# Half 0 of a mixing step computed by blocks of 16 rows instead of units of 8, with whole PSUM banks

## The chip, the core and the metric

The kernel runs on one core of one Trainium2 chip. The metric is the time of one execution on the device in microseconds (us); the figure for a version is the median of its runs. The core has five engines that run side by side, each with its own instruction stream: TensorE (PE, matrix products into PSUM), VectorE (DVE), ScalarE (ACT), GpSimd (POOL) and SyncE (SP, which here only issues DMA transfers). An engine waits for another by a semaphore.

## The reference

The function takes an image `x` of 256 rows x 256 columns x 128 channels and runs two layers on it, each as `x + layer(groupnorm(x))`. Layer 0 is gated attention along each row. Layer 1 treats the 256 rows of the first axis as 256 *tokens*, each an image of 256 x 128 pixels, and does this, cut to what matters here:

```python
tok_n = instance_norm(tokens)
k, q  = fno_layer(tok_n, ...), fno_layer(tok_n, ...)   # low resolution
v     = fno_layer(tok_n, ...)                          # full resolution
probs = softmax(q k^T)                                 # 8 heads, 256 x 256 each
attn  = probs v                                        # tokens mixed, every pixel
attn  = fno_layer(attn, p_wr, p_wi, p_bias, p_sw, p_sb)
attn  = instance_norm(attn + tokens)
...                                                    # two more FNO layers on groups of 4 tokens
```

An `fno_layer` is a 1 x 1 skip product plus a product in a few low Fourier modes, turned back into an image. The kernel has folded the attention heads, the value and output skips and the residual into one 256 x 256 matrix over the tokens (`mpT`), and all that passes through modes into a small set of modes (`Gd0`, in DRAM). What the stage of the change computes is therefore

    y = rwb * (mpT . x1 + inverse transform of the modes Gd0)

for all 256 tokens and all 32768 pixels, and, for each token, the statistics (mean and variance) of y, which the next normalisation needs. `x1` is the output of layer 0, `rwb` a row of 128 factors over the image column.

## The kernel before

Layer 0 takes about the first 1650 us of the execution and isn't touched. Layer 1 works on two halves of 128 tokens, half 0 and half 1, with one token per partition. After the attention matrix is made, `y_blocks(0, ...)` computes y of half 0 and leaves it in SBUF (`blocks`, 16 blocks of 2048 pixels a token; `hb[b]` is block b). Then the first spectral stage of half 0 (`first_modes`) runs interleaved with `y_blocks(1, ...)`, which computes y of half 1 and stores it to DRAM (`yd`). The later stages follow.

All of this is in a `manual_schedule`: on each engine the instructions stand in the order in which the Python code issues them, SP's DMAs among them. Nothing is reordered by a scheduler. Tiles come from pools; a tile with `bufs=3` has three buffers that are used in turn, and an instruction that takes a buffer over waits until the last reader of its former content is done.

A *unit* u of `y_blocks` is 8 rows of the 256 x 128 image (1024 pixels); a block is two units. For each unit:

- `load(u + 2)` issues on SP the DMAs of unit u + 2: x1 of both token halves, `xt`, 2 x 512 KB, three buffers (`load_x1`, L1017), and for an even unit the modes of its block, `gs`, 4 x 64 KB, three buffers (`load_modes`, L1248).
- Four PSUM tiles `yps_..._j` are taken from a pool of 8 banks of 512 columns (pool `psy`). Each uses the first 256 columns of its bank. Tile j holds the rows n with n mod 4 = j (`by_turn`).
- Mixing matmuls (L1351): for each j and each token half sc one product of `mpT` (128 x 128) with 256 pixels of `xt`. They use the whole 128 x 128 array. In the profile each appears as two instructions, so a unit has 16.
- `image` (L1219): for each of the unit's two rows per tile, and each j, the inverse transform along one row, of 32 modes into 128 columns. These matmuls use a row tile of 32 of the array; the four j use four different tiles. Again 16 instructions a unit in the profile.
- DVE multiplies each of the four tiles by `rwb` into `blocks` (L1361, 128 x 256 each) and takes the statistics of the unit's 1024 pixels in two `bn_stats` (L1363, 512 each).

When all 32 units are done, the pool `psy` is closed, and its banks pass to the pool `pz`, from which `y_blocks(1, br, ...)` and `first_modes` take theirs (four banks each). The first DVE instruction of `first_modes` is the aggregate of the statistics (`bn_aggr`, L1451). The image matmuls of later stages come from the same function `image`, there with four rows at a time, as do `first_images` (tiles `ups`) and `output` (tiles `h2ps`).

## Time and profile before

| | |
|---|---|
| median of 3 runs | 2884.54 us (2880.02 to 2887.79) |
| profiled execution | 2878.79 us, of it the span of the profile 2877.0 us |
| mean granted TensorE clock | 0.957 |
| busy in the span: PE, DVE, POOL, ACT | 92%, 70%, 58%, 52% |
| half 0 of y, first matmul to first matmul of half 1 | 1892.67 to 2032.05 us |

The span runs from the first to the last instruction of the profiled execution. All times inside it are counted from its start. The page divides it into 40 slices of 72 us and gives for each the busy share of an engine in tenths (9 is 90% or more); the stage of the change lies in slices 27 to 29:

```profile
PE   7799999999999999999999989999889988799655
DVE  7788888888888888888888854756645555365445
ACT  0477777777777777777777622200004611365132
POOL 0399999999999999999999900200114733111211
PEclk9999999999999999999999999999999999799865
DMA  9422222222222222222222101188879984798599
```

`DMA` is the mean busy share of the 16 DMA engines. The matmuls are pipelined, and their ends are modelled, so what tells the pace of PE is when one group starts after another, not the busy time of one. In lines of the costs and the timeline, "x16" is the number of instructions, and the time in brackets is how long the engine stood idle before the first of them, with what ended it.

### The profile page before, as it was taken

What the parts mean: (1) busy time and instruction counts of PE and PEld (TensorE: products, weight loads), DVE (VectorE), ACT (ScalarE), POOL (GpSimd) and SP (SyncE); (2) the same over time, 40 slices, a digit from 0 to 9 for tenths busy, and PEclk for the clock granted to TensorE, in tenths of its full rate; (3) what the DMA queues carried; (4) which work ended last, traced back from release to release, by engine and by line L of the source; (5) the groups of instructions that cost most, each with busy time, mean ns of one, the idle gap of its engine ahead of it and who ended that gap; (6) DMA issues with size and microseconds to landing.
All of it is one profiled execution on the core that took longest, in us unless ns stands there. A gap on an engine that the chain in (4) does not pass through costs nothing. (4 is left out here: it accounts for less than half of the span.)

```text
span 2877.0 us, 71481 instructions
## 1 busy us (share of the span) xinstructions
PE 2643.1 (92%) x29116; PEld 1935.1 (67%) x29116; DVE 2004.2 (70%) x3264; ACT 1488.4 (52%) x2847; POOL 1679.6 (58%) x1308
## 2 busy tenths in 40 slices
PE   7799999999999999999999989999889988799655
PEld 6677777777777777777777656778665555455533
DVE  7788888888888888888888854756645555365445
ACT  0477777777777777777777622200004611365132
POOL 0399999999999999999999900200114733111211
PEclk9999999999999999999999999999999999799865
DMA  9422222222222222222222101188879984798599
GB/s 369 166 67 67 67 67 67 67 67 67 68 67 67 67 67 67 67 67 67 67 67 67 47 22 54 34 276 274 281 243 312 311 304 134 253 363 306 187 360 339
DMA packets 246705, 430.12 MB, mean 149 GB/s; under 512 B 26278, under 2 KB 174201, under 8 KB 239976
## 3 DMA queue, kind: packets, MB, share of 16 engines
q1 hardware_dynamic: 206568, 335.34, 35.4%
q0 software_dynamic: 22912, 81.80, 7.4%
q10 hardware_dynamic: 16896, 8.39, 1.0%
q8 instruction: 231, 3.78, 0.6%
q14 instruction: 98, 0.80, 0.1%
HBM read 290.17 MB, written 135.27 MB: 148 GB/s over the span
## 5 line engine op out<-in xcount | busy, mean ns | idle before, releaser
L332 POOL TENSOR_TENSOR e<-e,b1T 128x1024 f32<-128x1024 f32 x256 | 606.1, 2367 | 164.6 <-PE u L381 90.3
L336 POOL TENSOR_TENSOR es<-e 128x512 f32<-128x512 f32 x512 | 639.6, 1270 | 20.1
L314 ACT ACTIVATE sc<-sc,b2T 128x512 f32<-128x512 f32 x512 | 339.0, 662 | 364.6 <-PE sc L305 356.2
L356 DVE RECIPROCAL av<-av 128x256 f32<-128x256 f32 x256 | 452.3, 1767 | 27.2 <-DVE og L355 1.4
L314 ACT ACTIVATE e<-sc,b2T 128x512 f32<-128x512 f32 x512 | 348.6, 681 | 0.0
L327 DVE TENSOR_TENSOR e<-sc,b1T 128x1024 f32<-128x1024 f32 x256 | 311.0, 1215 | 0.0
L305 PE MATMUL sc<-qkT 32*128 32x256 f32 x4096 | 293.4, 400 | 1.3 <-DVE e L327 1.3
L344 PE MATMUL av<-e,v 128*32 128x256 f32 x4096 | 274.7, 385 | 0.5 <-POOL e L332 0.5
L305 PEld LDWEIGHTS sc<-qkT 32*128 32x128 f32 x4096 | 185.1, 184 | 112.2 <-issue 97.7
L1351 PE MATMUL yps<-xt,mpT 128*128 128x256 f32 x1024 | 241.8, 389 | 19.4 <-DVE yt L1361 9.7
L355 DVE SCALAR_TENSOR_TENSOR og<-gate,av 128x256 f32<-128x256 f32 x256 | 107.7, 421 | 190.6 <-PE av L349 190.6
L1351 PEld LDWEIGHTS yps<-xt,mpT 128*128 128x128 f32 x1024 | 191.9, 192 | 56.7 <-DVE yt L1361 13.0
L1365 POOL DMA_DIRECT2D yd<-yt x32 | 17.7, 555 | 340.8 <-DVE yt L1361 340.8
L360 POOL TENSOR_TENSOR x<-xt,bo 128x256 f32<-128x256 f32 x256 | 187.7, 734 | 0.0
L279 PE MATMUL qk<-xnT,wT_wq 128*128 128x256 f32 x512 | 179.5, 432 | 1.7 <-ACT xnT L271 1.7
L285 PEld LDWEIGHTS gv<-wT_wv,kvT 128*128 128x128 f32 x1024 | 155.0, 192 | 13.3
L349 PE MATMUL av<-es,ones 128*32 128x256 f32 x2048 | 157.5, 379 | 2.5 <-POOL es L336 2.5
L366 PE MATMUL wo<-wT_wo,og 128*128 128x128 f32 x1024 | 156.8, 276 | 2.7 <-DVE og L357 2.7
L344 PEld LDWEIGHTS av<-e,v 128*32 128x32 f32 x4096 | 107.0, 109 | 76.1 <-POOL e L332 1.0
L381 PE MATMUL u<-adft,x 128*128 128x129 f32 x1024 | 156.4, 275 | 0.0
L285 PE MATMUL gv<-wT_wv,kvT 128*128 128x128 f32 x1024 | 156.0, 275 | 0.0
L1718 ACT ACTIVATE blocks<-h2ps,col 128x512 f32<-128x512 f32 x128 | 89.0, 779 | 129.4 <-PE h2ps L1219 129.4
(546 smaller groups left out, 5282.8 us busy)
## 6 DMA issues: line engine op xcount, KB each, us to landing
xt<-x1d SPq DMA_DIRECT2D x128, 512.0 KB, 5.9
xb<-in_x_dram SPq DMA_DIRECT2D x32, 1024.0 KB, 7.8
xt<-in_x_dram SPq DMA_DIRECT2D x128, 256.0 KB, 2.7
kt<-in_L_conv_kv_x_dram SPq DMA_DIRECT2D x128, 256.0 KB
x1d<-x SPq DMA_DIRECT2D x256, 128.0 KB, 2.3
y<-yd SPq DMA_DIRECT2D x62, 512.0 KB, 8.9
gs<-Gd SPq DMA_DIRECT2D x384, 64.0 KB, 5.1
yd<-yt POOLq DMA_DIRECT2D x32, 512.0 KB, 6.3
```

Source lines behind the costliest of these rows:

```text
L279: nc.tensor.matmul(ps[:, 0:256], wT["wq"], xnT, start=True, stop=True)
L285: nc.tensor.matmul(ps[:, 256 + c * P : 256 + (c + 1) * P], kvT[:, c * P : (c + 1) * P], wT["wv"], start=True, stop=True,)
L305: nc.tensor.matmul(sc[h // 2][:, h % 2, c * 256 : (c + 1) * 256], qkT[p, 256 + c * P : 256 + (c + 1) * P], qkT[p, 0:256], start=True, stop ...
L314: nc.scalar.activation(r["e"][1][:, :, c, :] if hp else z, z, AF.Exp, bias=b2T[:, c, s : s + 1])
L327: nc.vector.tensor_tensor(r["e"][0].rearrange("p h c q -> p (h c q)"), r.pop("sc").rearrange("p h x -> p (h x)"), b1T[:, 0:2].rearrange("p ...
L332: nc.gpsimd.tensor_tensor(e1, e1, b1T[:, 2:4].rearrange("p h c q -> p (h c q)"), ALU.mult)
L336: nc.gpsimd.tensor_tensor(r["es"][hp], e[:, :, 0, :], e[:, :, 1, :], ALU.add)
L344: nc.tensor.matmul(ps[hd, 0:256], r["v"][:, c, hd], r["e"][h // 2][:, h % 2, c, :], start=(c == 0), stop=(c == 1),)
L349: nc.tensor.matmul(ps[32 * h : 32 * h + 32, 256:512], self.ones, r["es"][h // 2][:, h % 2, :], start=True, stop=True,)
L356: nc.vector.reciprocal(rd, rd)
L360: nc.gpsimd.tensor_tensor(r["x1"], r["x"], bc(self.bo, 1, 2), ALU.add)
L1351: nc.tensor.matmul(rows_of(ps[j]), mpT[:, sc, tt], by_turn(xt[:, sc])[:, j], start=(sc == 0), stop=False,)
```

## The change

`y_blocks(0, ...)` is replaced by a function of its own for half 0, which works by blocks of 16 rows:

- A block takes four PSUM tiles of 512 columns, whole banks. The mixing matmuls of its first unit write columns 0 to 255 of each, those of its second unit columns 256 to 511. Only the very first product into a bank has the start flag.
- `image` then runs once a block over all four rows of each tile.
- DVE multiplies four tiles of 128 x 512 a block and takes the four `bn_stats` after them. The number of products falls from 128 to 64; the number of `bn_stats` stays 64.
- The modes of block b + 1 are requested at the start of block b, ahead of the x loads of units 2b + 2 and 2b + 3. Before, they were requested behind the x load of the first of these. The number and the size of the DMAs are the same.
- There are as many matmuls as before, on the same operands. Half 1 still uses `y_blocks`.

```diff
+        def y_half_0(psum):
+
+            tt = slice(0, P)
+            gss = {}
+
+            def modes(b):
+                gss[b] = xp.tile([P, 4, P], FP, tag="gs", name=f"gs_0_{b}", bufs=3)
+                load_modes(gss[b], Gd0, b, tt)
+
+            modes(0)
+            for b in range(16):
+                if b < 15:
+                    modes(b + 1)
+                for u in (2 * b + 2, 2 * b + 3):
+                    if u < 32 and (0, u) not in xts:
+                        xts[0, u] = load_x1(0, u)
+                gs = gss.pop(b)
+                ps = [psum.tile(f"yps_0_{b}_{j}") for j in range(4)]
+                for s in range(2):
+                    xt = xts.pop((0, 2 * b + s))
+                    for j in range(4):
+                        for sc in range(2):
+                            nc.tensor.matmul(
+                                rows_of(ps[j])[:, 2 * s : 2 * s + 2], mpT[:, sc, tt], by_turn(xt[:, sc])[:, j],
+                                start=(s == 0 and sc == 0), stop=False,
+                            )
+                image(ps, gs, bsy)
+                for j in range(4):
+                    nc.vector.tensor_tensor(by_turn(hb[b])[:, j], rows_of(ps[j]), bc(rwb, 1, 4), ALU.mult)
+                for g in range(4):
+                    nc.vector.bn_stats(ystat[:, 0, 4 * b + g, :], hb[b][:, g * 512 : (g + 1) * 512])
+
@@
             with tc.tile_pool(name="psy", bufs=8, space=PSUM) as psy:
-                run(y_blocks(0, Banks(psy, "y"), 0, 32))
+                y_half_0(Banks(psy, "y"))
```

In the changed file the lines of half 0 are L1390 (mixing matmuls), L1396 (the product on DVE) and L1398 (the statistics), and all lines below the new function stand 32 further down.

## The prediction

> **What bounds the kernel now.** One core, so the page and its 40 slices come first, to find where the change lies. Then the waits and the costs by line of that stretch, then the timeline of two of its units, then the timeline of its end, and last the transfers.

> The changed code runs from 1892.67 us (the first L1351 matmul) to 2032.05 us (the first matmul of half 1). In the busy times by stretch this stage reads:

> ```profile
> 1892.67:2030.55 137.88, 137.88 (x1024) 111.77 (x1024) 84.25 (x188) 0.00 (x0) 0.00 (x0) 1.00 0.87 278
> ```

> The columns are length, then busy us for each engine, the granted clock, the DMA share. PE is busy in all of the 137.88 us at full clock. DVE works 84 of them, ACT and POOL nothing. So PE sets the pace here, with DMA (87%) next. The waits of the same stretch say the same:

> ```profile
> DVE blocks L1361 <- PE yps L1219: 52.6, 32, 4.1
> PEld yps L1219 <- issue: 10.6, 32, 0.3
> PEld yps L1351 <- DVE blocks L1361: 1.7, 1, 1.7
> PE yps L1351 <- DVE blocks L1361: 1.5, 1, 1.5
> ```

> DVE waits for PE in each of the 32 units. PE waits for DVE once, at the end, and never for a transfer. The second line is the one to remember: at the start of each unit's image matmuls the weight load stands still for 0.33 us, 32 times. The timeline shows one unit:

> ```profile
> 1927.10 3.72 PE L1351 MATMUL yps<-xt,mpT 128*128 128x256 f32 x16
> ...
> 1930.75 0.54 PEld L1219 LDWEIGHTS yps<-bsy,gs 32*128 32x128 f32 x16 [0.33 <-issue]
> 1930.76 0.73 PE L1219 MATMUL yps<-bsy,gs 32*128 32x128 f32 x16
> 1930.86 5.11 SPq L1017 DMA_DIRECT2D xt<-x1d  x4
> 1931.41 3.32 PEld L1351 LDWEIGHTS yps<-xt,mpT 128*128 128x128 f32 x16
> 1931.41 3.72 PE L1351 MATMUL yps<-xt,mpT 128*128 128x256 f32 x16
> ```

> A unit takes 4.31 us: mixing matmuls (L1351) from 1927.10, image (L1219) from 1930.76, the next unit's mixing from 1931.41. So the mixing phase is 3.66 us and the image phase 0.65 (the trace counts each matmul of the source twice, hence 16). Each x load is issued 0.10 us after the mixing matmuls of the unit that held its buffer end.

> [...] The mixing matmuls use the whole array (128*128), the image ones four row tiles (32*128), so each unit switches twice. [...] The trace has 416 (L1361) and 687 (L1192, 128x512 from PSUM), and these are used. [...]

> **The change, part by part.**

> *Fewer mode switches (gain).* A block of two units now runs 32 mixing instructions, then 32 image ones: one pair of switches where there were two. What a pair costs follows from two undisturbed rows. Just ahead of the stage, L1187 runs the same 128*128 128x256 matmuls without a switch, and its DVE consumer starts each 8 of them:

> ```profile
> 1887.52 0.69 DVE L1192 TENSOR_TENSOR Fy<-Z,fyps 128x512 f32<-128x512 f32 x1 [1.04 <-PE fyps L1187]
> 1889.25 0.69 DVE L1192 TENSOR_TENSOR Fy<-Z,fyps 128x512 f32<-128x512 f32 x1 [1.04 <-PE fyps L1187]
> ```

> 1.73 us for 8 is 0.216 each. Sixteen would take 3.45, the unit takes 3.66: 0.21 us go to the two ends. For the image side, first_images runs it with four rows:

> ```profile
> 2214.08 1.17 PE L1219 MATMUL ups<-k_bsyn,gs 32*128 32x128 f32 x32
> 2215.18 1.96 PE L1572 MATMUL htps<-ident,blocks 128*128 128x128 f32 x16
> ```

> 1.10 us from its start to the next whole-array matmul, against 2 x 0.65 = 1.30: 0.20 less. After the change a block should take 2 x 3.66 - 0.21 + 1.10 = 8.21 us in place of 8.62: 0.41 us saved, times 16 blocks = 6.6 us. Bounds: if long runs don't keep the 0.216 spacing, only the image side stays, 16 x 0.20 = 3.2; if the 0.33 us idle of the weight load and 0.17 at the way back all go, 8.0. I take 6.6, for both rows are the same shapes.

> *Whole banks (DVE).* Per block 4 products of 128x512 replace 8 of 128x256. Four of 416 ns run in 1.42 us, so each starts 0.33 after the last, 0.08 less than its duration. Four of 687 should take 3 x 0.60 + 0.69 = 2.5 us, and the four statistics 2 x 1.29 = 2.58 as before: 5.1 against 5.42 us in a block of 8.21. PE hides it: 8 banks hold two blocks, so a block's banks have a whole block's 8.2 us to come free. Gain and cost nothing, except at the end.

> *The end of the stage (cost).* There nothing covers DVE:

> ```profile
> 2030.57 1.42 DVE L1361 TENSOR_TENSOR blocks<-yps,rwb 128x256 f32<-128x256 f32 x4 [1.57 <-PE yps L1219]
> ...
> 2032.05 3.72 PE L1351 MATMUL yps<-xt,mpT 128*128 128x256 f32 x16 [1.49 <-DVE blocks L1361]
> 2033.35 1.89 DVE L1451 BATCH_NORM_AGGREGATE col<-ystat 128x2 f32<-128x384 f32 x1
> ```

> The pool of half 1 takes over the banks of psy, and its first matmul starts 0.06 us after the last of the four products, not after the first: it waits for all. With 2.5 us in place of 1.42 the wait grows by 1.1. Behind the products stand four statistics instead of two (+1.29), then the aggregate (1.89): it ends 4.5 us after PE's restart, where half 1's first products, at 2036.44 us in the same timeline, could start at 4.39. About 0.1 us passes on to PE, which reuses those banks. Together -1.2. Bounds: 0, if banks are handed on one by one, to 2.4, if PE felt the statistics as well.

> *Loads.* SP issues the same DMAs in a new order: modes of block b+1, then x of units 2b+2 and 2b+3; before, the modes stood behind the even x load. The modes now wait behind the odd load of the block before, issued when a unit's mixing ends; their four issues (1.85 us) fit into the 3.45 until the next x buffer is freed, and they are asked for more than 15 us before use. So they delay no x load. But the time from freed buffer to use changes: before, each x load had two units and an image, 9.3 us. Now an even unit has 1.10 + 8.21 = 9.3, an odd one 3.45 + 1.10 + 3.55 = 8.1. Does a load take that long?

> ```profile
> 1926.55:1927.41 0.86, 0.86 (x17) 0.73 (x18) 0.22 (x1) 0.00 (x0) 0.00 (x0) 1.00 0.05 19
> ...
> 1934.29:1935.15 0.86, 0.86 (x8) 0.48 (x7) 0.00 (x0) 0.00 (x0) 0.00 (x0) 1.00 0.79 324
> 1935.15:1936.01 0.86, 0.86 (x17) 0.74 (x18) 0.20 (x1) 0.00 (x0) 0.00 (x0) 1.00 0.11 43
> ```

> Each of these stretches ends in its DMA share and GB/s. At both ends of 8.6 us the DMA engines are nearly idle (0.05, 0.11), just before an even load starts moving, so all issued earlier has landed, the odd load of 1930.86 within 4.4 us. Both leads suffice. Per block they work 0.87 x 8.62 = 7.5 us, and 8.21 is still more.

> *Sum.* 6.6 - 1.2 = 5.4 us. The profiled execution took 2878.8 us (span 2877.0 and 1.8 around it) and would take 2873.4. The median of three is 2884.5, 5.7 above it within a spread of 7.8, so the median after should be 2879.1.

> **The rivals.**

> *The gain is lost further on (0.13): 2884.5.* For it: the DMA share is 0.93 from 2190 to 2305 us and 0.99 from 2480 to 2630, so work that starts earlier could meet a resource that doesn't. Against: those transfers are issued into buffers that PE's progress frees, none starts before this stage, so they move with it.

> *More than forecast (0.10): 2875.* The switch saves the upper bound 8.0 and the end costs nothing, and a little more comes from transfers that interleave better later. For it only that the bounds allow it.

> *Slower: x arrives late (0.09): 2895.* From block 1 on, each odd unit waits for its x because the lead is 8.1 in place of 9.3 us. "No wait before" alone would allow a landing of up to 9.3. At 9.2 each of 15 blocks stalls 1.1 us: 16 us lost, less the 5.4. It decides from a stall of 0.36 us a block. The idle slices speak against it: landing would have to double because the modes now follow the odd load.

> **How the numbers follow.** The forecast has 0.68, with an own range of 2876 to 2884 (3.2 - 2.4 to 8.0 - 0). The range must also hold the spread of such medians and the first two rivals: 2871 to 2888 leaves out the slow case and some tail. A measurement of this kernel tells 0.3%, 8.7 us, from no change, so the forecast itself lies within "same". Faster by more: the second rival and 0.08 of the forecast's upper end, 0.18. Slower by more: the third rival and 0.01, 0.10. Same: 0.72.

> **What would show it.** Right: block period 8.2 us; the 0.33 us idle of the weight load 16 times in half 0, not 32; L1396 at about 687 ns x64; PE's wait for DVE at the end 2.6 us; the stage 131 us and half 1 starting near 2026.3. Wrong: PE waiting on a DMA of xt in odd units, a mixing phase above 7.2 us, or the stages after half 0 longer by as much as this one is shorter.

## The result, and the profile after

The changed kernel takes 2878.12 us (median of 22 runs, 2871.28 to 2885.2); the kernel before took 2882.3 us over as many runs. The ratio is 0.9985 with a 95% interval of 0.9978 to 0.9992: 4.3 us less, somewhere between 2.3 and 6.3.

The profiled execution of the changed kernel took 2885.2 us (span 2883.4), more than the one of before, although the median is lower. Single spans differ by more than the change is worth. So stages are compared here, each counted from its own start. Half 0 begins at 1895.43 us in the new trace. Its busy times, with the columns as in the prediction (length; busy us of PE, PEld, DVE, ACT, POOL with counts; granted clock; DMA share; GB/s):

```profile
1895.43:2026.70 131.27, 131.27 (x1024) 111.65 (x1024) 74.71 (x122) 0.00 (x0) 0.00 (x0) 1.00 0.91 291
```

131.3 us where there were 137.9, and PE is still busy in all of them. The timeline of one block (start, busy us, engine, line, operation, operands, count) shows why:

```profile
1928.23 7.17 PE L1390 MATMUL yps<-xt,mpT 128*128 128x256 f32 x32
1928.32 2.48 DVE L1396 TENSOR_TENSOR blocks<-yps,rwb 128x512 f32<-128x512 f32 x4 [3.22 <-PE yps L1219]
1930.83 2.47 DVE L1398 BATCH_NORM_STATS2 ystat<-blocks 128x6 f32<-128x512 f32 x4
...
1935.33 1.17 PE L1219 MATMUL yps<-bsy,gs 32*128 32x128 f32 x32
...
1936.44 7.17 PE L1390 MATMUL yps<-xt,mpT 128*128 128x256 f32 x32
```

From 1928.23 to 1936.44 is 8.21 us for a block; the mixing phase lasts 7.10 us, the image phase 1.11. DVE is done with a block 5.1 us after its image and then waits 3.2 us for the next. The waits of the stage (us in total, times, longest):

```profile
DVE blocks L1396 <- PE yps L1219: 56.2, 16, 8.0
PEld yps L1219 <- issue: 6.0, 18, 0.3
...
PEld yps L1351 <- DVE blocks L1396: 2.7, 1, 2.7
PE yps L1351 <- DVE blocks L1396: 2.6, 1, 2.6
```

The weight load's idleness of 0.33 us is there 16 times for half 0 (the other two belong to half 1), and PE waits for no transfer. The wait at the end has grown from 1.5 to 2.6 us, as forecast. What follows it was not forecast:

```profile
2026.81 2.48 DVE L1396 TENSOR_TENSOR blocks<-yps,rwb 128x512 f32<-128x512 f32 x4 [3.22 <-PE yps L1219]
2029.32 2.47 DVE L1398 BATCH_NORM_STATS2 ystat<-blocks 128x6 f32<-128x512 f32 x4
...
2029.35 5.41 PE L1351 MATMUL yps<-xt,mpT 128*128 128x256 f32 x16 [2.56 <-DVE blocks L1396]
2031.83 1.89 DVE L1483 BATCH_NORM_AGGREGATE col<-ystat 128x2 f32<-128x384 f32 x1
...
2034.68 0.73 PE L1219 MATMUL yps<-bsy,gs 32*128 32x128 f32 x16
```

The first unit of half 1 needs 5.33 us from its first matmul to its image (2029.35 to 2034.68). Before, it needed 3.65. No idleness stands inside it. The busy times by stretch tell what happened:

```profile
2028.00:2029.35 1.35, 0.01 (x1) 0.01 (x1) 1.32 (x4) 0.00 (x0) 0.00 (x0) 1.00 1.02 410
2029.35:2030.50 1.15, 1.15 (x3) 0.97 (x4) 1.15 (x2) 0.00 (x0) 0.00 (x0) 0.59 1.04 347
2030.50:2031.50 1.00, 1.00 (x4) 0.73 (x4) 1.00 (x3) 0.00 (x0) 0.00 (x0) 0.50 0.76 120
2031.50:2032.50 1.00, 1.00 (x4) 0.82 (x3) 0.96 (x2) 0.00 (x0) 0.00 (x0) 0.50 0.10 29
2032.50:2033.50 1.00, 1.00 (x5) 0.84 (x4) 1.00 (x1) 0.00 (x0) 0.00 (x0) 0.77 0.08 21
```

The granted clock (third number from the end) is 1.00 during the pause, falls to 0.50 at 2029.55 us, 0.2 us after PE starts again, and comes back 3.41 us later, at 2032.96. In that time the mixing instructions start 0.43 us apart (2029.77, 2030.19, 2030.62), twice the 0.22 us of full clock. PE's own speed, not a wait, costs the 1.68 us. The busy share of PE shows nothing of it: PE is busy throughout. After the end of half 0, then, two costs stand against the gain: the longer wait, and the half clock behind it.

### The profile page after: what moved, and what is told of

It is laid out like the page before. It is cut to its first block, busy times and chain, and to the rows that moved or that the text cites. A ratio compares the mean times of both kernels' runs of the same rounds, so it can differ in the third digit from the quotient of the medians.

```text
span 2883.4 us, 71403 instructions
## 1 busy us (share of the span) xinstructions
PE 2647.9 (92%) x29116; PEld 1943.0 (67%) x29116; DVE 1999.8 (69%) x3200; ACT 1487.9 (52%) x2847; POOL 1682.3 (58%) x1308
## 5 line engine op out<-in xcount | busy, mean ns | idle before, releaser
L291 DVE COPY v<-gv 128x256 f32<-128x256 f32 x256 | 108.6, 424 | 68.8 <-PE gv L289 68.8
L289 PE MATMUL gv<-xnT,wT_wg 128*128 128x256 f32 x512 | 153.4, 381 | 0.0
```

## The experiments

All times of this table are counted from the first mixing matmul of half 0. "Unit 0, length" is the time from the first matmul of half 1 to the image of that unit; "clock" is the mean granted clock over this time (over the first 4 us of it, it is 0.57 in the changed kernel, and this is the figure in the expectations below). Units 1 and 2 are the next two of half 1; "spectral" is the first `rhops` matmul of `first_modes`, which needs the aggregate of the statistics; "ups" is the first image matmul of `first_images` (tiles `ups`). The ratio is to the kernel before, run on the same chip.

| version | half 1 starts | unit 0, length | clock | unit 1 starts | unit 2 starts | spectral | ups | ratio [95%] |
|---|---|---|---|---|---|---|---|---|
| before | 139.38 | 3.65 | 1.00 | 144.25 | 150.06 | 159.63 | 298.63 | |
| changed | 133.92 | 5.33 | 0.68 | 140.48 | 146.29 | 155.86 | 299.47 | 0.9985 [0.9978, 0.9992] |
| e1_image_by_unit | 140.43 | 3.65 | 1.00 | 145.31 | 151.12 | 160.69 | 299.25 | 1.0003 [0.9992, 1.0015] |
| e2_modes_behind | 133.91 | 5.34 | 0.68 | 140.47 | 146.29 | 155.86 | 294.08 | 0.9984 [0.9974, 0.9995] |
| e8_pe_kept_busy | 133.96 | 3.62 | 1.00 | 138.81 | 144.62 | 154.20 | 292.43 | 0.9982 [0.9973, 0.9990] |
| e4_last_by_unit | 133.25 | 3.65 | 1.00 | 138.13 | 143.94 | 153.51 | 291.90 | 0.9973 [0.9960, 0.9986] |
| e6_no_seam | 131.29 | 3.65 | 1.00 | 136.74 | 141.62 | 157.01 | 294.21 | 0.9970 [0.9958, 0.9982] |
| e9_last_by_unit_no_seam | 131.70 | 3.65 | 1.00 | 136.78 | 142.59 | 152.18 | 290.71 | 0.9966 [0.9954, 0.9979] |

The theory at the start: the switches between the two tile shapes (128\*128 and 32\*128) carry the whole gain, and the end of the stage gives part of it back, by the wait and by the clock. The rivals: the gain comes from elsewhere (whole banks on DVE, the order of the DMAs), or the slow unit is slow for another reason than PE's pause.

**Is it the switches?** e1_image_by_unit keeps the change but runs the image of each unit behind that unit's mixing.

```diff
                 for s in range(2):
                     ...
+                    for k in (2 * s, 2 * s + 1):
+                        for j in range(4):
+                            q = slice(32 * j, 32 * j + 32)
+                            nc.tensor.matmul(
+                                ps[j][:, k * W : (k + 1) * W], gs[q, k, :], bsy[q, :], start=False, stop=(k == 3)
+                            )
-                image(ps, gs, bsy)
```

> The changed kernel, with the image matmuls of each unit set back behind that unit's mixing matmuls; whole banks, four 128x512 products a block and the modes one block ahead stay. Theory (the gain is the switch of the array's tiling mode, once a block in place of twice): a block takes 8.6 us again, half 0 some 138 us up to the wait at its end, the weight load idles 0.33 us 32 times in half 0, and PE still waits 2.6 us at the end; the time is 1 us above the kernel before, ratio 1.000 to 1.001. Rival (the gain is the whole banks or the earlier modes): a block stays at 8.2 us, ratio 0.9985.

The ratio is 1.0003 [0.9992, 1.0015]: all the gain is gone. Its timeline:

```profile
2025.84 3.72 PE L1390 MATMUL yps<-xt,mpT 128*128 128x256 f32 x16
...
2029.49 0.73 PE L1397 MATMUL yps<-bsy,gs 32*128 32x128 f32 x16
...
2030.15 3.72 PE L1390 MATMUL yps<-xt,mpT 128*128 128x256 f32 x16
...
2033.80 0.73 PE L1397 MATMUL yps<-bsy,gs 32*128 32x128 f32 x16
...
2037.08 3.72 PE L1351 MATMUL yps<-xt,mpT 128*128 128x256 f32 x16 [2.56 <-DVE blocks L1401]
...
2040.73 0.73 PE L1219 MATMUL yps<-bsy,gs 32*128 32x128 f32 x16
```

4.31 us a unit again, 8.62 a block, and the weight load's 0.33 us 32 times again:

```profile
PEld yps L1397 <- issue: 10.6, 32, 0.3
```

So the switches are the gain, and the whole banks by themselves cost the 1.05 us by which half 1 starts later than before (140.43 against 139.38). One thing did not fit: PE pauses for the same 2.56 us here, yet unit 0 takes 3.65 us at full clock. The last section returns to it.

**Are the earlier modes worth anything?** e2_modes_behind puts them back behind the even x load.

```diff
-                if b < 15:
-                    modes(b + 1)
                 for u in (2 * b + 2, 2 * b + 3):
                     if u < 32 and (0, u) not in xts:
                         xts[0, u] = load_x1(0, u)
+                    if u % 2 == 0 and b < 15:
+                        modes(b + 1)
```

> The changed kernel with the modes of the next block requested behind the even x load, as the kernel before had it; all else as changed. Theory (the order of the loads is worth nothing, both leads suffice): a block takes 8.21 us, half 0 lasts 134 us from its first matmul to the first of half 1, no PE wait for a transfer in half 0; ratio to before 0.998 to 0.999 like the changed kernel. Rival (the earlier modes give part of the gain): PE waits for gs in half 0 and the stage is over 135 us.

```profile
1927.62 7.17 PE L1390 MATMUL yps<-xt,mpT 128*128 128x256 f32 x32
...
1935.83 7.17 PE L1390 MATMUL yps<-xt,mpT 128*128 128x256 f32 x32
```

8.21 us a block, half 1 at 133.91 instead of 133.92, ratio 0.9984: the order of the loads is worth nothing. The half clock is there again (5.34 us).

**Is the slow unit slow because PE paused?** e8_pe_kept_busy fills the pause with five products (ten instructions) into a PSUM bank of their own, whose result nobody reads.

```diff
+            warm = psum.tile("warm")
+            for k in range(5):
+                nc.tensor.matmul(warm[:, 0:256], ident, mpT[:, k % 2, :], start=True, stop=True)
```

> The changed kernel with five matmuls of 128x256 more (ten instructions, some 2.2 us) into a free bank behind the last image matmuls of half 0; their result isn't used. Theory (PE's clock halves because PE idles 2.56 us there): the granted clock stays at 1.0 over the end of the stage and the first unit of half 1 takes 3.65 us from its first matmul to its image in place of 5.33; the start of half 1 moves by at most 0.2 us. Rival (that unit is slow for its x, its modes or by chance): it takes 5.3 us as in the changed kernel. Total: 1.7 us less than the changed kernel, or the same.

```profile
2027.66 2.43 PE L1401 MATMUL warm<-mpT,ident 128*128 128x256 f32 x10
...
2030.33 3.69 PE L1351 MATMUL yps<-xt,mpT 128*128 128x256 f32 x16 [0.25 <-PE warm L1401]
...
2033.95 0.73 PE L1219 MATMUL yps<-bsy,gs 32*128 32x128 f32 x16
```

```profile
2030.33:2033.95 3.62, 3.62 (x16) 2.93 (x16) 3.58 (x5) 0.00 (x0) 0.00 (x0) 1.00 0.76 196
```

Half 1 starts at the same place (133.96), for DVE frees the banks no sooner, but the clock stays at 1.00 and unit 0 takes 3.62 us. DVE works beside it as before (3.58 of 3.62 us). So neither DVE nor the transfers slow the unit; the clock does. That the filling is what kept the clock at 1.00, this run alone doesn't show: the pause, left empty, might have been harmless here, as it was in e1 (see the last section). Unit 1 starts 1.67 us earlier than in the changed kernel. The ratio, 0.9982, can't be told from 0.9985: 1.7 us is 0.06%, less than either interval is wide. What is shown, is shown by the profile.

**Is the end worth repairing?** e4_last_by_unit keeps blocks 0 to 14 and does block 15 in two units, with 256-column products and two `bn_stats` each, so that DVE has only 1.42 us of products behind the last image.

```diff
-            for b in range(16):
+            for b in range(15):
...
+            for s in range(2):
+                xt = xts.pop((0, 30 + s))
+                ps = [psum.tile(f"yps_0_15_{s}_{j}")[:, 0:256] for j in range(4)]
...
+                image(ps, gss[15], bsy, range(2 * s, 2 * s + 2))
+                yt = hb[15][:, s * HB : (s + 1) * HB]
...
```

> The changed kernel, with its last block alone computed by units, two products of 128x256 sets of four and two pairs of statistics, as the kernel before had it. Theory (the end of the stage costs what DVE still has to do after the last matmul): PE's wait there falls from 2.56 to 1.5 us, the block costs 0.4 us more, so 0.7 us less by that alone; if the half clock that followed the 2.56 us of idleness in the changed kernel's profile comes from the length of that idleness, the first unit of half 1 takes 3.65 us again in place of 5.33, another 1.7 us less. Ratio to before 0.9976 to 0.9983. Rival (half clock by chance, or for another reason): first unit of half 1 at 5.3 us or mixed.

```profile
2025.55 3.72 PE L1351 MATMUL yps<-xt,mpT 128*128 128x256 f32 x16 [1.49 <-DVE blocks L1409]
...
2029.20 0.73 PE L1219 MATMUL yps<-bsy,gs 32*128 32x128 f32 x16
```

The wait is 1.49 us as before the change, and with it the half clock is gone too (3.65 us). Half 1 starts 0.67 us earlier than in the changed kernel (1.07 of wait less 0.41 for one pair of switches more), unit 1 2.35 us earlier. Ratio 0.9973 [0.9960, 0.9986].

**Without the hand-over of banks.** The wait exists because pool `psy` must be done before `pz` takes its banks: in the changed kernel the first matmul of half 1 starts 0.06 us after the last product of block 15 (2026.81 + 2.48). e6_no_seam opens `pz` first and lets half 0 use its two sets of four banks in turn. Half 1 then starts in the four that came free a block earlier. One unit of half 1 is issued ahead of `first_modes`.

```diff
-            with tc.tile_pool(name="psy", bufs=8, space=PSUM) as psy:
-                y_half_0(Banks(psy, "y"))
             pz = _Held(tc.tile_pool(name="pz", bufs=4, space=PSUM))
             bq, br = Banks(pz.pool, "q"), Banks(pz.pool, "r")
+            y_half_0((br, bq))
...
-                ps = [psum.tile(f"yps_0_{b}_{j}") for j in range(4)]
+                ps = [psum[b % 2].tile(f"yps_0_{b}_{j}") for j in range(4)]
...
                     y1 = y_blocks(1, br, 0, U1)
+                    next(y1)
+                    next(y1)
```

> The changed kernel without a wait between the halves: half 0 takes its banks from the two pools of the following stages, blocks in turn from one and the other, so that the first unit of half 1 finds its banks free; and the first unit of half 1 stands ahead of the aggregate of half 0's statistics on DVE. Theory (the end of the stage is the other term of the sum): PE waits less than 0.2 us at the end of half 0 and about 1 us one unit later, the clock stays at 1.0, the third unit of half 1 starts 2 to 4 us earlier than in the changed kernel; ratio to before 0.997 to 0.998. Rival (what is saved there is lost later, on the chain of first_modes or on transfers): half 1 ends no earlier than in the changed kernel, ratio 0.9985.

```profile
2023.38 3.72 PE L1351 MATMUL yps<-xt,mpT 128*128 128x256 f32 x16
...
2028.83 3.72 PE L1351 MATMUL yps<-xt,mpT 128*128 128x256 f32 x16 [1.08 <-DVE yt L1361]
...
2031.01 1.87 DVE L1483 BATCH_NORM_AGGREGATE col<-ystat 128x2 f32<-128x384 f32 x1
```

Unit 0 starts without a wait. Unit 1 waits 1.08 us for DVE, which works off the products of unit 0 behind the four statistics of block 15. Unit 2 is 4.67 us ahead of the changed kernel, but the aggregate now stands behind a unit of half 1 on DVE, so the spectral stage starts 1.15 us later (157.01 against 155.86). The ratio is 0.9970 [0.9958, 0.9982]. Not all of the lead lasts: at "ups" e6 stands at 294.21, no earlier than e2 (294.08), which has both the wait and the half clock. That is the sign of the rival, loss further on, so the profile doesn't explain why the ratio is lower than that of the changed kernel, and the two intervals overlap.

**Both repairs.** e9_last_by_unit_no_seam joins the last block by units with the shared banks, and leaves the aggregate where it was.

```diff
+            y_half_0((bq, br))
...
-                ps = [psum.tile(f"yps_0_{b}_{j}") for j in range(4)]
+                ps = [psum[b % 2].tile(f"yps_0_{b}_{j}") for j in range(4)]
...
+                ps = [psum[1 - s].tile(f"yps_0_15_{s}_{j}")[:, 0:256] for j in range(4)]
```

> The changed kernel with its last block by units and the banks taken in turn from the two pools of the next stages, so that half 1 finds its banks free and only half a block stands on DVE behind the last matmul; the aggregate stays where it was. Theory (both terms of the end are removed): half 0 to half 1 131.7 us, second unit of half 1 at 136.7 us after the start of half 0 (138.1 in the kernel with the last block by units alone, 140.5 in the changed one), rhops at 152 us; the clock stays at 1.0; ratio to before 0.9965 to 0.998, 1 to 2 us better than with the last block by units alone. Rival (the aggregate on DVE takes the place of the wait for banks): the second unit no earlier than 138 us.

```profile
2026.59 3.72 PE L1351 MATMUL yps<-xt,mpT 128*128 128x256 f32 x16
2026.67 1.42 DVE L1409 TENSOR_TENSOR blocks<-yps,rwb 128x256 f32<-128x256 f32 x4 [0.99 <-PE yps L1219]
...
2029.45 1.89 DVE L1496 BATCH_NORM_AGGREGATE col<-ystat 128x2 f32<-128x384 f32 x1
...
2031.25 1.35 DVE L1361 TENSOR_TENSOR yt<-yps,rwb 128x256 f32<-128x256 f32 x4
...
2031.67 3.72 PE L1351 MATMUL yps<-xt,mpT 128*128 128x256 f32 x16 [0.70 <-DVE yt L1361]
```

PE passes from half 0 to half 1 without a pause. The first products of half 1 stand behind the aggregate and start 0.35 us after their matmuls are done (2030.24 + 0.66), so unit 1 waits 0.70 us instead of the usual 0.50. The spectral stage starts at 152.18, 7.5 us ahead of before and 3.7 ahead of the changed kernel. The ratio is 0.9966 [0.9954, 0.9979], a median of 2871.32 us: this beats the kernel before, and it is the best of the versions by its median and in the profile up to the spectral stage. Its interval just overlaps that of the changed kernel.

**What brings the half clock?** e1 had shown a pause of 2.56 us without it. There PE had spent only 0.65 us in 32-row image matmuls ahead of the pause, not 1.1. So a theory was made, the author's guess, that the image phase counts as idleness together with the pause. e10_last_image_by_unit gives block 15 alone the short image phase of e1; e11_one_more_matmul puts one product (two instructions) on the whole array behind the last image, and shortens the pause to 1.98 us. Both were single profiles.

```diff
+                    if b == 15:
+                        for k in (2 * s, 2 * s + 1):
...
-                image(ps, gs, bsy)
+                if b < 15:
+                    image(ps, gs, bsy)
```

> The changed kernel, with the image matmuls of its last block alone set back behind each unit, so that 16 image instructions instead of 32 stand before the end. PE still idles 2.56 us there. Three profiles with 32 image instructions before that idleness (changed kernel twice, modes behind once) show the clock at 0.5 for 3.4 us after it; the one with 16 (image by unit) shows 1.0. Theory [...]: clock 1.0, the first unit of half 1 takes 3.65 us, half 0 to half 1 134.3 us. Rival (2.56 us of idleness alone is enough, image by unit kept its clock by chance): 0.57 again and 5.3 us.

```diff
+            warm = psum.tile("warm")
+            for k in range(1):
+                nc.tensor.matmul(warm[:, 0:256], ident, mpT[:, k % 2, :], start=True, stop=True)
```

> The changed kernel with one matmul of 128x256 more (two instructions, some 0.5 us) into a free bank behind the last image matmul; its result isn't used. PE then idles some 2.1 us. Theory [...]: clock 1.0, first unit of half 1 3.65 us. Rival (any long pause after the image matmuls brings the half clock): 0.57 again, 5.3 us.

```profile
2028.39 5.20 PE L1351 MATMUL yps<-xt,mpT 128*128 128x256 f32 x16 [2.56 <-DVE blocks L1405]
```

```profile
2028.67 5.32 PE L1351 MATMUL yps<-xt,mpT 128*128 128x256 f32 x16 [1.98 <-issue]
```

Both are slow (the first line is e10, the second e11; unit 0 takes 5.14 and 5.25 us). So that theory falls: a short image phase didn't save the clock here, nor did two whole-array instructions ahead of a pause of 1.98 us. The first 3.33 us of unit 0 in e11 run at half clock:

```profile
2028.67:2032.00 3.33, 3.33 (x8) 2.71 (x9) 3.30 (x5) 0.00 (x0) 0.00 (x0) 0.50 0.64 164
```

**The two kernels once more.** a2_after_again and b2_before_again are the unchanged texts, profiled a second time.

> The changed kernel once more, for what varies between profiles. Half 0 to half 1 133.9 us as in its first profile. If the half clock after the 2.56 us of idleness comes by chance (the kernel with the image by unit idles 2.56 us as well and kept 1.0), it may be absent here: then the first unit of half 1 takes 3.65 us and the first ups stands 5 to 6 us earlier than in the kernel before, at 292 to 294 us after the start of half 0. If it belongs to the change, 5.3 us again.

> The kernel before once more, for what varies between profiles. Half 0 to half 1 139.4 us as in its first profile; if the half clock at the end of half 0 needs PE idle for over 1.5 us, the clock stays at 1.0 there; the first ups some 298 to 299 us after the start of half 0.

The seam repeats to 0.02 us: half 1 at 133.91 and unit 0 of 5.32 us at clock 0.68 after, 139.37 and 3.65 us at 1.00 before. What doesn't repeat is "ups": 294.05 in the second profile of the changed kernel, 299.47 in the first. The first has one event in half 1 that no other profile has, a late transfer and the half clock after it, 14 instructions in 6.21 us:

```profile
2177.20 6.21 PE L1351 MATMUL yps<-xt,mpT 128*128 128x256 f32 x14 [1.94 <-DMA xt<-x1d]
```

Before, "ups" stands at 298.63 and 300.91. Against these, the changed kernel without that event (294.05, and 294.08 in e2) keeps 4.6 to 6.9 us of lead there. So the gain isn't lost between half 0 and `first_images`.

## Why the prediction was right, and where its sum was off

The forecast was 2879.1 us, the result 2878.12; "same" by its bound of 0.3%, as it said. The closeness is partly luck: the base of three runs, 2884.5, lies 2.2 us above the median of 22, and the gain was put at 5.4 instead of 4.3 us.

- **Fewer mode switches, 6.6 us: right.** A block takes 8.21 us exactly as worked out from the two rows. From the first matmul of half 0 to PE's stop is 131.36 us (2029.35 - 2.56 - 1895.43) against 137.88: 6.52. e1 shows that this is all of the gain. A pair of switches costs 0.41 us here (8.62 - 8.21). The runs show this price, not what it consists of.
- **Whole banks on DVE, nothing except at the end: right.** DVE needs 5.1 us of 8.21 and waits in every block.
- **Loads, nothing: right.** PE waits for no transfer in half 0, and e2 gives the same block period with the old order. The rival "x arrives late" is excluded.
- **The end of the stage, -1.2 us: the mis-sized term.** The wait itself is right, 2.56 us, 1.07 more. The 0.1 us said to pass on through the aggregate isn't there: unit 1 waits 0.50 us before and after the change, and in e8 too, where unit 0 runs at full clock and leaves the aggregate no more time than was assumed. What the term left out is the half clock after the longer pause, 1.68 us: it took for granted that PE goes on at full speed. In both profiles of the changed kernel, the end costs 1.07 + 1.68 = 2.75 us, a little beyond the bound of 2.4, which had been set by DVE's statistics.
- **Sum.** 6.52 - 1.07 - 1.68 = 3.77 us, which is just what unit 2 of half 1 gains (150.06 - 146.29). It agrees with the 4.3 [2.3, 6.3] of the runs; 5.4 lies inside that interval too, so it is the profile that corrects the term, not the runs.
- **Half 1 near 2026.3:** the terms of the sum give 2032.05 - 6.6 + 1.1 = 2026.55 in before's trace, so the figure was a slip; measured is 1892.67 + 133.92 = 2026.59.
- **L1396 at 687 ns:** the median of the 64 is 680.
- **The other rivals.** "Lost further on" is not what happened (the lead at "ups"); "more than forecast" asked for 8.0 us from the switches.

## What to carry to other kernels

In this kernel, matmuls of two tile shapes were cheaper in long runs of one shape (8.21 us a block against 8.62): price one pair of switches from two rows of the profile that run without them, and multiply. When a stage is made coarser, look at its last piece, where nothing covers the engine behind PE (PE's wait there grew from 1.49 to 2.56 us); do that piece in the old size (1.49 us again in e4), or let the next stage start in buffers that are already free (no wait in e6 and e9). And price a pause of PE as more than its length where the trace shows half clock behind it: here a pause lengthened by 1.07 us cost another 1.68 behind it. It didn't in every version: e1 paused for the same 2.56 us and kept full clock, as the next section shows.

## What the hardware did that was not expected

```profile
2026.14:2029.55 3.41, 0.85 (x25) 0.66 (x20) 2.71 (x5) 0.00 (x0) 0.00 (x0) 1.00 1.01 384
2029.55:2032.96 3.41, 3.41 (x9) 2.70 (x9) 3.38 (x5) 0.00 (x0) 0.00 (x0) 0.50 0.57 144
```

```profile
2032.46:2035.88 3.42, 2.07 (x23) 1.44 (x21) 1.33 (x3) 0.00 (x0) 0.00 (x0) 1.00 0.90 265
2035.88:2039.29 3.41, 2.21 (x10) 1.98 (x11) 3.38 (x6) 0.00 (x0) 0.00 (x0) 1.00 1.01 345
```

The second number behind the times is PE's busy time. In the changed kernel the whole pause lies in one stretch, PE is idle for 2.56 of its 3.41 us, and the next stretch runs at half clock. In e1 a border cuts the pause into 1.35 and 1.21 us, and the clock stays at 1.00. The border lies 0.21 us behind PE's restart in the changed kernel and 1.20 us ahead of it in e1. All profiles of this place, by the idleness within one stretch:

| profiles | pause of PE | most of it within one stretch | unit 0 |
|---|---|---|---|
| e6, e9 | none | | full clock |
| e8 | 0.25 | 0.25 | full clock |
| before | 1.49 | 0.94 | full clock |
| e1 | 2.56 | 1.35 | full clock |
| before again, e4 | 1.49 | 1.49 | full clock |
| e11 | 1.98 | 1.87 | half at first, 5.25 us |
| e10 | 2.56 | 2.18 | half at first, 5.14 us |
| changed twice, e2 | 2.56 | 2.55 to 2.56 | half at first, 5.32 to 5.34 us |

The two rows next to the step, e4 and then e11:

```profile
2023.88:2027.30 3.42, 1.93 (x16) 1.57 (x9) 3.15 (x7) 0.00 (x0) 0.00 (x0) 1.00 1.00 368
2025.15:2028.56 3.41, 1.54 (x34) 1.02 (x30) 2.48 (x4) 0.00 (x0) 0.00 (x0) 1.00 1.02 395
```

So e4 kept its clock with a shorter pause, and e1 with one of 2.56 us that a border cuts. In e8 a border stands at 2028.77 us; the pause, unfilled, would have run from 2027.73 to 2030.33 and been cut into 1.04 and 1.56 us (an estimate from the lines of that run).

Nor is a stretch idle throughout where half clock followed: in e11 it was idle for 1.87 of 3.41 us. From 1700 to 2190 us of the traces of before and of the changed kernel, all eight full-clock stretches with more than 2 us of idleness (2.14 to 2.94) were followed by half clock, and of the 264 others (at most 1.63) one was. It is that of the late transfer above, with 1.57 us of idleness (2172.91 to 2176.33 us), while 1.63 us elsewhere left the clock full (before, 1853.62 to 1857.03 us). So idle time alone doesn't tell the two cases apart; what else counts there stays open.
